# A list scheduler for two graph layers on one core: other durations, delays and port rules, hence another order of the same instructions

## The chip, the core and the metric

The kernel runs on one core of a Trainium2 chip. The core has a matrix engine (TensorE, in the profile PE, with its weight loads on a line of their own, PEld), a vector engine (VectorE, DVE), a scalar engine with activation functions (ScalarE, ACT), a general engine (GpSimd, POOL) and a sync engine (SyncE, SP), which here issues the transfers. Each engine runs its own list of instructions in order; semaphores make one wait for another. The metric is the device time in microseconds of one execution; the median of three runs of the kernel before is 2105.4 us (2105.02 to 2105.88).

## What is computed

There are 128 graphs of 128 nodes with 256 features each, x of shape (128, 128, 256) in f32, and an adjacency matrix of integers per graph. Two layers follow each other, each with a LayerNorm and ReLU ahead of it and a residual around it. The first is a gated graph network of three steps, the second a graph attention:

```python
# layer 0
h = relu(layernorm(x)); A = (adj != 0)
for i in range(3):
    m    = h @ weight[i]
    aggr = einsum('bst,bsd->btd', A, m)
    gi, gh = aggr @ w_ih.T + b_ih, h @ w_hh.T + b_hh      # three gates each
    r, z = sigmoid(i_r + h_r), sigmoid(i_z + h_z)
    n    = tanh(i_n + r * h_n)
    h    = (1 - z) * n + z * h
x = x + h
# layer 1
h = relu(layernorm(x)); Wh = h @ W; s = Wh.sum(-1)
e = leaky_relu(s[:, :, None] + s[:, None, :], 0.2); e = where(adj == 0, -inf, e)
x = x + softmax(e) @ Wh
```

## The kernel before, in words

**Tiling.** Four graphs make a group, and there are 32 groups. A group passes three phases, one for each step of the gated network, and then the attention. The list `turns` (L897 to L902) fixes the order of the phases; in the steady state it is (g, 0), (g − 1, 1), (g − 2, 2), so that three groups are under way at once. Three phases make a period.

**A phase.** The weights of a step are multiplied into w_ih beforehand, so the edge sums act on h itself: h is split into three bf16 parts, and `edge_sums` multiplies them with the adjacency matrix (L623, 12 bf16 matmuls of 128x128 for each half of the features), and ACT copies the sums out of the PSUM bank as `aT` (L626). The gate products use a fast multiplication scheme with seven products of halves: `node_sums` forms sums of halves, `hs` from the state on POOL and `gs` from the edge sums on DVE (L666 to L670), and `products` forms the seven products for two kinds of gates (`rz` and `n`) in six PSUM banks `x_`, `y_` and `q_`. In steps 0 and 1 a product is made of 128x256 matmuls (`product`, L697), in step 2, where rows come out directly, of 128x384 ones (`product_rows`, L711). `products` writes their order out: x (1), q (5), y (6), y (7), x (2), y (4), q (3), each for `rz` and then for `n`; in step 2 the middle numbers differ. Between them ACT copies banks out with `put` (L743; L747 and L749 where a bias is added), and DVE adds q to those copies with `add` (L753). The bank y_rz is such a loop: product (6) on it, ACT's copy L743 of it, then product (7) on the same bank; y_n (6) lies between. `gru` (L799 to L823) and `gru_rows` (L849 to L893) turn the sums into gates and the new state.

**Transposes.** Where the other layout of the state is needed, ACT copies halves of the f32 words into `pl` (L559) or `pe` (L1163), SP issues a transposing transfer, and ACT copies the result back (L563).

**Attention.** It is spread over the phases of later groups: e from the scores (L1022, L1040, or L1044 and L1046), exponentials on ACT (L1055), transposes, the weighted sums of rows (`weighted`, L652), the product with W (L1088) and the division and the residual on DVE (L1097). The last two groups have forms of their own (L993 to L1015, L1073, L1120 to L1149).

**The planner.** All of that is recorded first: `Plan.op` takes an engine, a duration in ns, the function that emits the instructions, and the buffers read and written. `Plan.run` is a list scheduler. It gives every operation a rank (its due time less durations and lags on the way there), and then places one operation after another on a clock for each engine: each time it takes the engine whose operation can start earliest, and among those the lowest rank. The gate products have due times, and their order among themselves is fixed (`bound`); all other TensorE work is put between them where it fits. A result becomes visible on another engine `LAG` ns after its end; DVE operations marked `two` and all of POOL's exclude each other in a reckoned `port`. The clocks serve only to find an order: at the end the operations are emitted in the order in which they were placed, and the engines run them as fast as their semaphores let them.

The functions that the change touches are these:

Of the kernel before, what the change touches and what calls it, by code (L numbers as in the profile page):

```python
# [13 lines left out]
OP = mybir.AluOpType  # L14
# [27 lines left out]
class Plan:  # L42
# [7 lines left out]
    LAG = {"PE": 250, "ACT": 300, "DVE": 300, "POOL": 300, "SP": 4000}  # L50
# [20 lines left out]
    def op(self, eng, ns, fn, reads=(), writes=(), room=(), due=None, mark=None,  # L71
           turn=None, two=False, lag=None):
# [24 lines left out]
        for b in free:  # L97
# [3 lines left out]
                           two or eng == "POOL", self.LAG[eng] if lag is None else lag])  # L101
# [4 lines left out]
        if turn is not None:  # L106
            self.turns.append((i, turn))

    def run(self):
# [29 lines left out]
        def rank_all():  # L139
            for i in reversed(topo):  # L140
                eng, ns, due = nodes[i][0], nodes[i][1], nodes[i][5]
                gap = 0 if i in bound else MARGIN
                rank[i] = min([due] + [rank[u] - (0 if nodes[u][0] == eng != "SP" else nodes[i][7])
                                       - (gap if u in bound else 0) for u in after[i]]) - ns
# [15 lines left out]
        clock, port = dict.fromkeys(self.LAG, 0.0), 0.0  # L160
# [3 lines left out]
        while len(order) < len(nodes):  # L164
            best = None
            for e, pool in ready.items():
# [3 lines left out]
                for i in pool:  # L170
                    if i in bound and i != chain[-1]:
                        continue
                    t = max(clock[e], at[i], port if nodes[i][6] else 0.0)
# [5 lines left out]
                    starts.append((t, i))  # L179
                first = min((t for t, _ in starts), default=float("inf"))  # L180
                if first == float("inf"):
                    continue
                i = min((i for t, i in starts if t <= first), key=lambda i: (rank[i], i))
                if best is None or first < best[0]:
                    best = (first, e, i)
            t, e, i = best
# [4 lines left out]
            clock[e] = t + n[1]  # L191
            if n[6]:
                port = clock[e]
            end = max(end, clock[e])
            for b in n[4]:
# [6 lines left out]
                b.done = max(getattr(b, "done", 0.0), clock[e] + n[7])  # L202
                if not b.left:
                    slots[b.tag][b.slot[1]] = b.done
            for u in users[i]:
                missing[u] -= 1
                at[u] = max(at[u], clock[e] + (0 if nodes[u][0] == e != "SP" else n[7]))
# [8 lines left out]
def kernel(  # L216
# [281 lines left out]
    def normed(src, dst, lo=0, hi=G):  # L498
# [3 lines left out]
        for b in range(lo, hi):  # L502
            op("DVE", 415, lambda b=b: nc.vector.bn_stats(ap(st)[:, b, :], ap(src)[:, b, :]),
               [(src, b, b + 1)], [(st, b, b + 1)])
# [4 lines left out]
        op("DVE", 160 * (hi - lo), aggr, [st], [mv])  # L509

        def rstd():
# [3 lines left out]
        op("DVE", 170, lambda: nc.vector.scalar_tensor_tensor(  # L515
            ap(nm)[:, part], ap(mv)[:, part, 0], -1.0, ap(rs)[:, part], op0=OP.mult, op1=OP.mult),
           [mv, rs], [nm])
        for b in range(lo, hi):
            op("ACT", 520, lambda b=b: nc.scalar.activation(
# [31 lines left out]
    def turned_halves(src, rows, dst):  # L551
# [5 lines left out]
        for k in range(KD):  # L557
# [5 lines left out]
            op("ACT", 1340, lambda k=k: nc.scalar.copy(  # L563
# [3 lines left out]
    def transpose(pl, plT, k, n):  # L567

        op("SP", 100, lambda: nc.sync.dma_start_transpose(
            ap(plT)[:, k, 0:n].rearrange("p c (m q) -> p (c m) q", q=P),  # L570
            ap(pl)[:, k, 0:n].rearrange("p c m -> p (c m)")), [(pl, k, k + 1)], [(plT, k, k + 1)],
           lag=4500)

    def parts_of(rows):
# [3 lines left out]
        for n in range(2):  # L578
            part = slice(2 * n, 2 * n + 2)
            op("POOL", 1106, lambda part=part: nc.gpsimd.tensor_tensor(  # L580
                ap(r1)[:, part], ap(rows)[:, part], top(rows)[:, part], OP.subtract),
               [(rows, 2 * n, 2 * n + 2)], [(r1, n, n + 1)])
            op("POOL", 1050, lambda part=part: nc.gpsimd.tensor_tensor(  # L583
# [5 lines left out]
    def turned_parts(hT):  # L589
# [6 lines left out]
        for k in range(KD):  # L596
# [3 lines left out]
            op("POOL", 1150, lambda k=k, r=r: nc.gpsimd.tensor_tensor(  # L600
# [4 lines left out]
            op("POOL", 1150, lambda k=k, r=r: nc.gpsimd.tensor_tensor(  # L605
# [5 lines left out]
    def edge_sums(parts, a, dst):  # L611
# [5 lines left out]
        for k in range(KD):  # L617
# [7 lines left out]
            op("PE", 700, edges, reads(k) + [a], [ps], [dst])  # L625
# [18 lines left out]
    def weighted(m, a, dst, lo, hi, homes):  # L644

        n, cols = hi - lo, slice(lo * N, hi * N)
        for k in range(KD):
# [7 lines left out]
            op("PE", 225 * n, sums, [(m, lo, hi), (a, lo, hi)], [ps], [dst])  # L655
# [60 lines left out]
    def products(layer, hT, hs, aT, gs, rows=False):  # L716
# [23 lines left out]
        def put(t, y, bias=None, mark=None):  # L740
# [9 lines left out]
            op("ACT", 760, halves, [y, W["bias_n"]], [t], mark=mark)  # L750
# [37 lines left out]
    def gru(layer, hT, hs, aT, gs):  # L788
# [7 lines left out]
        for j, n, src in blocks:  # L796
            cr, cz, cn, i = j, KD + j, 2 * KD + j, 2 * j + n
            s_rz, nn = src["rz"], src["n"]
            op("ACT", 511, lambda j=j, n=n, s_rz=s_rz, c=cr: nc.scalar.activation(  # L799
                view(rz, 0)[:, j, n, :], ap(s_rz)[:, 0, :], AF.Tanh, bias=ap(W["bias_s"])[:, c:c + 1],  # L800
                scale=0.5), [s_rz, W["bias_s"]], [(rz, i, i + 1)])
            if src is X:
                op("DVE", 290, lambda j=j, n=n: nc.vector.tensor_scalar(
                    view(rz, 0)[:, j, n, :], view(rz, 0)[:, j, n, :], 1.0, None, op0=OP.add),
                   [], [(rz, i, i + 1)])
                op("DVE", 480, lambda j=j, n=n, nn=nn: nc.vector.scalar_tensor_tensor(
                    view(u)[:, j, n, :], ap(nn)[:, 0, :], ap(W["bias_n"])[:, 0:1], view(rz, 0)[:, j, n, :],
                    op0=OP.add, op1=OP.mult), [nn, (rz, i, i + 1), W["bias_n"]], [(u, i, i + 1)])
            else:
                op("DVE", 480, lambda j=j, n=n, nn=nn: nc.vector.scalar_tensor_tensor(  # L810
# [6 lines left out]
            op("ACT", 500, lambda j=j, n=n, s_rz=s_rz, c=cz: nc.scalar.activation(  # L817
# [18 lines left out]
    def gru_rows(layer, hT, hs, aT, gs, rows, x1):  # L836
# [6 lines left out]
        for j, n, src in blocks:  # L843
            i = 2 * n + j
            outs = slice(j * P, (j + 1) * P)
            for m, bank in enumerate((src["rz"], src["n"])):
                graph, unit_of = 2 * n + m, 2 * i + m
                sbuf = bank.tag[0] == "t"
                op("ACT", 390, lambda outs=outs, graph=graph, bank=bank: nc.scalar.activation(  # L849
# [3 lines left out]
                op("DVE", 290, lambda outs=outs, graph=graph, bank=bank: nc.vector.scalar_tensor_tensor(  # L853
# [4 lines left out]
                op("DVE", 290, lambda outs=outs, graph=graph, bank=bank: nc.vector.scalar_tensor_tensor(  # L858
                    view(u)[:, graph, outs], view(u)[:, graph, outs], 0.5, flat(bank)[:, 3 * P:4 * P],
                    op0=OP.mult, op1=OP.add), [bank], [(u, unit_of, unit_of + 1)], two=sbuf)  # L860
        for n in (1, 0):
# [5 lines left out]
            tanh = [723, lambda cols=cols: nc.scalar.activation(  # L867
# [19 lines left out]
            op("POOL", 1290, lambda cols=cols, part=part: nc.gpsimd.tensor_tensor(  # L887
# [20 lines left out]
    def group(g):  # L908
# [4 lines left out]
        for t, src, kb in ((rows0, x[graphs].rearrange("b n d -> n b d"), 512),  # L913
# [3 lines left out]
            else:  # L917
                op("SP", 100, lambda t=t, src=src: nc.sync.dma_start(ap(t), src), [], [t])
        op("DVE", 420, lambda: nc.vector.tensor_scalar(ap(a), ap(at), 0.0, None,
                                                       op0=OP.not_equal), [at], [a])  # L920
        plan.due = (phase(g, L - 1) + 2) * SLOT
        normed(rows0, rows0)
        for layer in range(L):
# [9 lines left out]
            else:  # L933
# [3 lines left out]
                op("SP", 100, lambda: nc.sync.dma_start(  # L937
                    ap(x1), x[graphs].rearrange("b n d -> n b d")), [], [x1])
            hs, aT, gs = buf("hs"), buf("aT"), buf("gs")
            node_sums(hT, hs, "POOL", 1390, 940)  # L940
            edge_sums(parts, a, aT)
            node_sums(aT, gs, "DVE", 690, 440)
# [12 lines left out]
    def edges_of(g, a):  # L955

        e = buf("e")
        op("DVE", 415, lambda: nc.vector.tensor_scalar(
            ap(e), ap(a), 0.0, -BIG, op0=OP.is_equal, op1=OP.mult), [a], [e])
        return e, (buf("s_all") if g >= NG - ENDING else e)  # L960

    def attention(g, scores, x1, h1, lo, hi):
# [8 lines left out]
        for b in range(lo, hi):  # L971
            hw = buf("hw")
            op("DVE", 520, lambda b=b, hw=hw: nc.vector.scalar_tensor_tensor(
# [65 lines left out]
        if ending:  # L1039
            op("DVE", cost, lambda: nc.vector.tensor_reduce(small(top), sums(), AX.X, OP.max), units, [top])  # L1040
            op("DVE", 260, bound, [s], [top, low])
            op("ACT", 320 * n, leaky, [s] + units, [(e, lo, hi)])
# [17 lines left out]
        op("ACT", (400 if ending else 320) * n, exps, [low],  # L1060
# [143 lines left out]
```

## Time and profile before

| what | value |
|---|---|
| runs, median of three | 2105.4 us |
| profiled execution, span from the first to the last instruction | 2103.8 us |
| TensorE busy | 2084.5 us (99%), 10,624 matmuls and transposes |
| DVE busy | 1714.1 us (81%) |
| ACT busy | 1612.9 us (77%) |
| POOL busy | 923.7 us (44%) |
| mean granted TensorE clock | 0.998 of full speed |
| transfers | 65 GB/s in the mean |
| rows load, issue to landing | 4.2 us (median of 32) |
| transposing transfers `plT`, issue to landing | 3.3 us (median of 186) |

Busy times are sums of instructions as they lie in the trace; consecutive matmuls overlap in it, so a busy TensorE is not one at its peak. The page's row of forty digits gives the busy share of each fortieth of the span in tenths (52.6 us each). A line of a timeline gives the start in us from the span's start, the busy time in us, the engine, the line of the kernel, the operation, output and inputs by name, the shape, and how many such instructions follow each other; in brackets stands how long the engine was idle just before, and what it was waiting for.

### The profile page before, as it was taken

The numbers are of one execution on the slowest core, as the hardware profiler recorded it, in microseconds if no ns is written. First come the engines' busy times: TensorE is split into PE (matmuls) and PEld (weight loads), VectorE is DVE, ScalarE is ACT, GpSimd is POOL, SyncE is SP. The second block draws the span as 40 slices with busy tenths as digits, with TensorE's granted clock in tenths as the row PEclk, the third lists the DMA queues.
The fourth block names the chain that finished last, engine by engine and source line by source line (L and its number), as shares of the span: only waits on it lengthen the run. The fifth ranks groups of instructions, "written<-read, shape, count | busy, mean of one in ns | idle before, by whom it ended". The sixth has DMA issues, their size and how long they took to land.

```text
span 2103.8 us, 30718 instructions
## 1 busy us (share of the span) xinstructions
PE 2084.5 (99%) x10624; PEld 1661.6 (79%) x10624; DVE 1714.1 (81%) x3626; ACT 1612.9 (77%) x2977; POOL 923.7 (44%) x881
## 2 busy tenths in 40 slices
PE   8999999999999999999999999999999999999998
PEld 6886887777887778887778877778877788688765
DVE  6767888788888888888888887888878978778788
ACT  5577887877878787877778777778787777677676
POOL 4544554344443435543444543444444454335330
PEclk9999999999999999999999999999999999999999
DMA  4322323322233222323223233222323222312231
GB/s 131 61 51 48 56 54 81 67 54 61 68 73 81 60 58 65 72 70 76 61 56 70 68 73 68 54 61 68 74 61 85 45 62 71 76 41 61 56 71 41
DMA packets 365148, 137.02 MB, mean 65 GB/s; under 512 B 296384, under 2 KB 364736, under 8 KB 364992
## 3 DMA queue, kind: packets, MB, share of 16 engines
q1 hardware_dynamic: 364992, 135.05, 28.8%
q8 instruction: 84, 1.38, 0.3%
q14 instruction: 72, 0.59, 0.1%
HBM read 45.36 MB, written 16.78 MB: 30 GB/s over the span
## 4 chain that ended last, share of the span: by engine, by line
PE 94%; DVE 3%; ACT 1%; DMA 1%; issue 0%; SPq 0%; DVEq 0%; ACTq 0%
PE y_rz L697 15%; PE q_rz L697 10%; PE x_rz L697 10%; PE y_n L697 8%; PE misc L623 6%; PE y_n L711 5%; PE y_rz L711 5%; PE x_n L697 5%; PE q_n L697 5%; PE misc L1088 5%; PE q_rz L711 4%; PE x_n L711 4%; PE x_rz L711 4%; PE q_n L711 4%; PE misc L652 3%; PE misc L452 0%
## 5 line engine op out<-in xcount | busy, mean ns | idle before, releaser
L580 POOL TENSOR_TENSOR r<-rows 128x512 f32<-128x512 f32 x126 | 139.7, 1129 | 295.9 <-ACT rows L563 201.7
L743 ACT COPY t_rz<-y_rz 128x512 f32<-128x512 f32 x192 | 112.5, 586 | 130.4 <-PE y_rz L697 91.8
L666 POOL TENSOR_TENSOR hs<-hT 128x512 f32<-128x512 f32 x96 | 126.6, 1319 | 190.7 <-PE y_n L711 110.9
L753 DVE TENSOR_TENSOR t_rz<-t_rz,q_rz 128x512 f32<-128x512 f32 x192 | 131.5, 685 | 86.5 <-ACT t_rz L743 43.5
L697 PE MATMUL y_rz<-hs,s_hh 128*128 128x256 f32 x768 | 197.4, 379 | 0.6 <-ACT t_rz L743 0.5
L697 PE MATMUL y_rz<-gs,s_x 128*128 128x256 f32 x768 | 197.1, 379 | 0.0
L670 POOL TENSOR_TENSOR hs<-hT,hs 128x256 f32<-128x256 f32 x96 | 77.5, 807 | 209.6 <-PE q_n L711 169.2
L697 PEld LDWEIGHTS y_rz<-gs,s_x 128*128 128x128 f32 x768 | 145.9, 190 | 19.8
L605 POOL TENSOR_TENSOR pl<-d,pl 128x512 bf16<-128x512 f32 x64 | 76.1, 1193 | 191.9 <-ACT pl L603 191.7
L697 PEld LDWEIGHTS y_rz<-hs,s_hh 128*128 128x128 f32 x768 | 143.5, 190 | 20.0 <-ACT t_rz L743 1.4
L583 POOL TENSOR_TENSOR p<-r 128x512 bf16<-128x512 f32 x126 | 156.7, 1262 | 0.0
L753 DVE TENSOR_TENSOR t_n<-t_n,q_n 128x512 f32<-128x512 f32 x192 | 131.2, 683 | 30.4 <-PE q_n L711 13.0
L666 DVE TENSOR_TENSOR gs<-aT 128x512 f32<-128x512 f32 x96 | 87.8, 914 | 54.3 <-ACT aT L626 53.7
L697 PE MATMUL x_rz<-aT,s_x 128*128 128x256 f32 x512 | 131.4, 379 | 0.0
L697 PE MATMUL x_rz<-hT,s_hh 128*128 128x256 f32 x512 | 131.4, 379 | 0.0
L600 POOL TENSOR_TENSOR d<-hT,pl 128x512 f32<-128x512 f32 x64 | 82.6, 1293 | 97.2 <-ACT pl L598 91.5
L626 ACT COPY aT<-misc 128x512 f32<-128x512 f32 x190 | 110.4, 586 | 17.7 <-PE misc L623 13.0
L1088 PE MATMUL misc<-w,uT 128*128 128x256 f32 x480 | 115.1, 383 | 3.1 <-DVE x L1097 2.3
L697 PE MATMUL y_n<-hs,s_hh 128*128 128x256 f32 x384 | 114.3, 379 | 0.0
L697 PE MATMUL y_n<-gs,s_x 128*128 128x256 f32 x384 | 114.2, 379 | 0.0
L697 PEld LDWEIGHTS x_rz<-hT,s_hh 128*128 128x128 f32 x512 | 97.2, 190 | 19.3
L887 POOL TENSOR_TENSOR x<-x,u 128x512 f32<-128x512 f32 x60 | 79.4, 1342 | 69.8 <-DMA x<-in_x_dram 42.1
(286 smaller groups left out, 6324.4 us busy)
## 6 DMA issues: line engine op xcount, KB each, us to landing
rows<-in_x_dram SPq DMA_DIRECT2D x32, 512.0 KB, 4.2
x<-in_x_dram SPq DMA_DIRECT2D x32, 512.0 KB, 3.9
out_dram<-x SPq DMA_DIRECT2D x31, 512.0 KB, 2.9
at<-in_adj_dram SPq DMA_DIRECT2D x32, 256.0 KB, 2.8
plT<-pl SPq DMA_TRANSPOSE x186, 3.3
peT<-pe SPq DMA_TRANSPOSE x60, 3.1
e<-in_L_gnn_weight_dram SPq DMA_DIRECT2D x3, 256.0 KB, 3.1
rz<-in_L_gnn_w_ih_dram SPq DMA_DIRECT2D x2, 384.0 KB, 4.3
```

The lines of the kernel that those rows point to most:

```text
L580: op("POOL", 1106, lambda part=part: nc.gpsimd.tensor_tensor(ap(r1)[:, part], ap(rows)[:, part], top(rows)[:, part], OP.subtract), [(rows, ...
L583: op("POOL", 1050, lambda part=part: nc.gpsimd.tensor_tensor(ap(p3)[:, part], ap(r1)[:, part], top(r1)[:, part], OP.subtract), [(r1, n, n ...
L600: op("POOL", 1150, lambda k=k, r=r: nc.gpsimd.tensor_tensor(ap(r), ap(hT)[:, k], part(pl, k, 0), OP.subtract), [(hT, 2 * k, 2 * k + 2), (p ...
L623: nc.tensor.matmul(flat(ps)[:, b * N:(b + 1) * N], part(i, b, k), ap(a)[:, b, :], start=(i == 0), stop=(i == 2))
L626: op("ACT", 590, lambda k=k, ps=ps: nc.scalar.copy(ap(dst)[:, k, :], flat(ps)), [ps], [(dst, 2 * k, 2 * k + 2)])
L666: op(eng, cost, lambda: sub(ap(w)[:, 0:2, :], blocks()[:, 1::2, :], blocks()[:, 0:2, :], OP.subtract), [t], [(w, 0, 2)], two=True)
L697: nc.tensor.matmul(ap(bank)[:, half, :], ap(w)[:, i - 1, gate, :], source(i, t, sums), start=(first and c == 0 and m == 0), stop=False, sk ...
L711: op("PE", 645, lambda c=c, w=w, t=t, sums=sums: nc.tensor.matmul(flat(bank)[:, c * P:(c + 3) * P], source(i, t, sums)[:, m * N:(m + 1) * ...
L743: op("ACT", 590, lambda: nc.scalar.copy(ap(t), ap(y)), [y], [t], mark=mark)
L753: op("DVE", 690, lambda: nc.vector.tensor_tensor(ap(t), ap(t), ap(q), OP.add), [q], [t])
L887: op("POOL", 1290, lambda cols=cols, part=part: nc.gpsimd.tensor_tensor(part(x1), part(x1), ap(u)[:, cols], OP.add), [(u, 2 * lo, 2 * hi)] ...
L1088: nc.tensor.matmul(ap(ps)[:, b, :], ap(uT)[:, k, (m + b) * N:(m + b + 1) * N], ap(w1)[:, k, :], start=(k == 0), stop=(k == KD - 1))
```

## The change

No instruction is added or removed. `Plan` reckons with other numbers:

- The durations of many operations are other numbers of ns, and four more DVE operations count as users of the port (`two=True`).
- The lag of an operation is split: `LAG` belongs to the producer, `SIGNAL` to the engine that waits; between two TensorE operations there is none. SP's transfers get 480 ns on the queue (transposes 1,283), a lag of 3,600 (transposes 2,200).
- `OVER` lets the next operation of the same engine begin before the end of the one before it.
- An f32 product behind a `thin` operation (the bf16 edges) starts `FLIP` = 56 ns later.
- The port is handed on `HANDOFF` = 120 ns before the end of its user.
- A released buffer can be used 36 ns later, and of two engines that could start something equally early, the one is taken whose operation asked first.

```diff
-    LAG = {"PE": 250, "ACT": 300, "DVE": 300, "POOL": 300, "SP": 4000}
+    LAG = {"PE": 163, "ACT": 0, "DVE": 0, "POOL": 0, "SP": 3600}
+    OVER = {"PE": 0, "ACT": 103, "DVE": 84, "POOL": 42, "SP": 0}
+    FLIP, HANDOFF = 56, 120
+    SIGNAL = {"PE": 53, "ACT": 36, "DVE": 36, "POOL": 78, "SP": 28}
...
+    def wait(self, i, u):
+        a, b = self.nodes[i], self.nodes[u][0]
+        return 0 if a[0] == b == "PE" else a[7] + self.SIGNAL[b]
...
-                rank[i] = min([due] + [rank[u] - (0 if nodes[u][0] == eng != "SP" else nodes[i][7])
+                rank[i] = min([due] + [rank[u] - self.wait(i, u)
                                        - (gap if u in bound else 0) for u in after[i]]) - ns
...
-                    t = max(clock[e], at[i], port if nodes[i][6] else 0.0)
+                    t = max(clock[e] + (self.FLIP if thin and e == "PE" and not nodes[i][8] else 0), at[i])
...
-                    starts.append((t, i))
-                first = min((t for t, _ in starts), default=float("inf"))
+                    starts.append((max(t, port) if nodes[i][6] else t, t, i))
+                first = min((t for t, _, _ in starts), default=float("inf"))
...
-                i = min((i for t, i in starts if t <= first), key=lambda i: (rank[i], i))
-                if best is None or first < best[0]:
-                    best = (first, e, i)
+                asked, i = min(((r, i) for t, r, i in starts if t <= first), key=lambda x: (rank[x[1]], x[1]))
+                if best is None or (first, asked) < best[:2]:
+                    best = (first, asked, e, i)
...
-            clock[e] = t + n[1]
+            done = t + n[1]
+            clock[e] = done - self.OVER[e]
             if n[6]:
-                port = clock[e]
-            end = max(end, clock[e])
+                port = done - self.HANDOFF
+            if e == "PE":
+                thin = n[8]
...
-                b.done = max(getattr(b, "done", 0.0), clock[e] + n[7])
+                b.done = max(getattr(b, "done", 0.0), done + n[7] + 36)
...
-                at[u] = max(at[u], clock[e] + (0 if nodes[u][0] == e != "SP" else n[7]))
+                at[u] = max(at[u], done + self.wait(i, u))
```

Of the operations, a few that stand for all:

```diff
-        op("SP", 100, lambda: nc.sync.dma_start_transpose(
+        op("SP", 1283, lambda: nc.sync.dma_start_transpose(
...
-           lag=4500)
+           lag=2200)
...
-            op("PE", 700, edges, reads(k) + [a], [ps], [dst])
+            op("PE", 671, edges, reads(k) + [a], [ps], [dst], thin=True)
...
-            op("ACT", 760, halves, [y, W["bias_n"]], [t], mark=mark)
+            op("ACT", 728, halves, [y, W["bias_n"]], [t], mark=mark)
...
-            tanh = [723, lambda cols=cols: nc.scalar.activation(
+            tanh = [630, lambda cols=cols: nc.scalar.activation(
...
-            node_sums(hT, hs, "POOL", 1390, 940)
+            node_sums(hT, hs, "POOL", 1272, 730)
...
-            op("ACT", 400, lambda b=b: exps(b, b + 1), [low], [(e, b, b + 1), (den, b, b + 1)])
+            op("ACT", 480, lambda b=b: exps(b, b + 1), [low], [(e, b, b + 1), (den, b, b + 1)])
```

## The prediction

> **What bounds the kernel now.** I read the page from the top, then the waits of TensorE, the span cut into forty windows, and the timelines of TensorE, ScalarE (ACT) and VectorE (DVE) around each wait. On the page:
>
> ```profile
> span 2103.8 us, 30718 instructions
> PE 2084.5 (99%) x10624; PEld 1661.6 (79%) x10624; DVE 1714.1 (81%) x3626; ACT 1612.9 (77%) x2977; POOL 923.7 (44%) x881
> PE   8999999999999999999999999999999999999998
> PE 94%; DVE 3%; ACT 1%; DMA 1%; issue 0%; SPq 0%; DVEq 0%; ACTq 0%
> ```
>
> TensorE is busy in 99% of the span and carries 94% of the chain that ended last. What it does can't change, so the question is only how much time is not matmuls at full pace. Busy time can't tell that: the Trainium skill ("Perfetto Trace Analysis", Identifying the Most-Contended Engine) says that pipelined matmuls make matmul busy time a bad measure. So I take spacings from start to start in the timeline. At full pace they are 0.2156 us for 128x256 f32, 0.3225 for 128x384, 0.0556 for the bf16 edge matmuls, 0.111 for 128x128 f32; the skill ("TensorE: Matmul & The Clock Gate", Wait — 56ns, not 53.3ns?) gives 55.6 and 215.7 ns for the first two kinds, and the trace agrees. All 10,624 spacings at these values make 2059.5 us. The other 44.4 of the 2103.8 are: 5.7 ahead of the first and after the last matmul's start; 8.4 in 149 changes from bf16 to f32, median 0.056; about 30 in waits and slow stretches (9.0 start-up, 1.3 at 157–221 us, 1.35 at 1659–1772, 8.3 at 1799–1812, 1.3 at 1998–2051, 7.1 in the end, 2.2 in crumbs). From 430 to 1500 us nothing waits. The runs' median, 2105.4, lies 1.6 above the span; I work on the span and add 1.6.
>
> A bf16-to-f32 change in the TensorE timeline (first number start, second busy): after edges, two starts take 0.70, elsewhere 0.65.
>
> ```profile
> 1791.05 0.86 PE L711 MATMUL q_n<-s_x,gs 128*128 128x384 f32 x2
> 1791.75 0.81 PE L711 MATMUL y_rz<-s_hh,hs 128*128 128x384 f32 x2
> 1792.40 0.81 PE L711 MATMUL y_rz<-s_x,gs 128*128 128x384 f32 x2
> ```
>
> The big hole, same view:
>
> ```profile
> 1797.35 1.89 PE L1088 MATMUL misc<-w,uT 128*128 128x256 f32 x8
> 1801.59 3.65 PE L1088 MATMUL misc<-w,uT 128*128 128x256 f32 x8 [2.35 <-DVE x L1097]
> 1807.26 0.91 PE L711 MATMUL y_n<-s_hh,hs 128*128 128x384 f32 x2 [2.03 <-ACT t_n L743]
> 1808.72 1.48 PE L711 MATMUL x_rz<-s_hh,hT 128*128 128x384 f32 x2
> ```
>
> Two idles of 2.5 and 2.4 us (with the hand-over), and behind each some matmuls at half pace: eight in 3.65 instead of 1.89 (+1.7), then five of 0.64 instead of 0.32 (+1.6). The skill (the same page, Part 1: The HAM clock gate) says the clock halves after an idle window of about 3.4 us that runs free; here 2.35 idle was enough. What is late there is DVE: a row of 128x512 that takes 0.69 us took 1.53 twice (L1044, L1046), L668 took 1.14 instead of 0.43, while POOL worked. "SBUF — State Buffer" (Who interferes with whom) says that a DVE instruction with two SBUF inputs and a reading GpSimd instruction exclude each other for a whole instruction; these rows fit.
>
> Lastly the place where gate products have no other work between them: y_rz (product 6), y_n (6), y_rz (7). ACT copies y_rz out (L743) while y_n runs, and y_rz goes on:
>
> ```profile
> 180.60 0.59 PE L697 MATMUL y_n<-gs,s_x 128*128 128x256 f32 x2
> 181.03 1.10 PE L697 MATMUL y_rz<-hs,s_hh 128*128 128x256 f32 x4
> ...
> 221.35 1.13 PE L697 MATMUL y_rz<-hs,s_hh 128*128 128x256 f32 x4
> 222.32 1.03 PE L697 MATMUL y_rz<-gs,s_x 128*128 128x256 f32 x4
> ```
>
> Copy on time: four matmuls busy for 1.10 instead of 1.03, so about 0.08 lost. At 221.35 ACT came 0.22 late (it had just begun a 1.04 copy, L1163), and 0.20 + 0.10 were lost: after a stop the second pass pays 0.1 more. Before has two such bare loops in 64 phases; everywhere else edges, attention or sums stand between.
>
> **The change, part by part.** The instructions are the same in number and kind; only their order differs. I read the order that the changed planner writes (an order, without times), counted TensorE's work at the spacings above, and the other engines' at their rows' lengths less what successive instructions overlap.
>
> 1. *Changes of type* (the 56 ns that the planner now charges an f32 product behind `thin` edges). It puts edges one behind another: 149 changes become 97 or 98. 51 x 0.056 = −2.9.
>
> 2. *Bare loops* (PE's lag 250 becomes 163 + 36, ACT's 300 becomes 0 + 53). Four products are planned at 0.864 us; the old numbers wanted 250 + 590 + 300 = 1,140 ns for the copy between, so the planner put fillers there; the new want 842, so it fits. Bare y_rz–y_n–y_rz loops go from 2 to 35. Each has 4 matmuls x 0.2156 = 0.86 from y_n's first start, 1.079 from the last start on y_rz; needed are 0.415 to ACT's start, 0.586 for the copy, 0.053 back = 1.054. Slack: 25 ns. With ACT free, 33 x 0.08 = +2.6. In the steady pattern ACT's queue ahead of that copy is 3.80 us of work from its last forced start (L743 0.48, L1163 0.95, L747 0.37, L749 0.27, L563 1.20, L867 0.53), 0.51 before it is needed. Windows of 1.3 to 2.0 us (y_n to y_n, row products, the attention's L1097) also become more frequent, with 0.4 or more of slack: 0, covered by that slack; a third of them 0.1 late would cost 4.
>
> 3. *Fill.* At 201–203 us ACT put seeds (L738) before two evictions: 0.43 + 0.23 + 2 x 0.10 = 0.86 lost. In the new order enough stands between: −0.9.
>
> 4. *The hole and the stretch before* (port sharing, measured DVE and ACT times). Before: 1.2 at 1765–1772 (an y_rz wait 0.68 + 0.10, gs 0.39) and 8.3, 9.4 together. In the new order the nearest squeeze is ahead of an y_rz (7) at about 1756 us of TensorE's work: ACT has L563, four L519, L747, L749, L559, L823 and the t2 copies in front of L743. Added up, they end 2.3 to 3.0 us after TensorE needs them; a wait of 0.33 stands just before. I take 2.6 + 0.3 + 0.4 for second passes + 1.7 for one halved clock = 5.0, so −4.4. Bounds: hole as large as before (0), or no halving and little left (−7).
>
> 5. *Edges behind their transpose.* The planner's 1283 + 2200 makes 3.48 us; the timeline shows 3.1–3.2 from issue to landing for two planes and about 3.65 for three. Once (about 1875 us of work) only 2.2–2.5 us of TensorE's work stand between: +1.3. "DMA: Bandwidth & Descriptors" (Anatomy of one DMA) puts a fixed 2 us on completion; the transposes here show more. A queue change on SP costs nothing while loads have phases of slack; where one is late, as the rows load of 6.1 us (usual 4.2) before the hole, it belongs to item 4's bounds.
>
> 6. *2004–2014 us.* Edges follow edges on one bank, nothing between: 0.83 + 0.10, and gs 0.26 + 0.10; before lost 1.0 here: +0.3.
>
> 7. *The end.* TensorE's work ahead of the last gate product shrinks by 2.4: the 2.9 of item 1 less 0.45 of attention matmuls (L1015) drawn ahead; so item 1's −2.9 is replaced by −2.4. After that product before needs 28.6 us, with DVE nearly full. The new order has done these DVE pieces ahead of it: L1022 0.72, L1040 0.72, one L871 0.72, one L753 0.60, L958 0.31, L1035–1038 about 0.2, some 3.3; it puts four L1097 (0.4 each) before the second half's chain, of which I let 0.6 count: −2.7 (bounds −1.0, −4.4).
>
> 8. *Start-up.* Fillers are re-ordered round DMA waits: 0, hidden behind the weight loads (0.9 and 1.3 us waits stay); the 1.6 at 30.6 us (L533) may go, or a new one come: −1.5 to +1.
>
> Sum: −2.4 + 2.6 − 0.9 − 4.4 + 1.3 + 0.3 − 2.7 = −6.2. Span 2103.8 − 6.2 = 2097.6; with 1.6, 2099.2 us.
>
> **Rivals.**
> - *A, slower: ACT is late at the bare loops.* Speaks for it: slack of 25 ns, and one of before's two was 0.22 late at a cost of 0.30. Against: the 0.51 counted. With 0.22 late everywhere, 33 x 0.30 = 9.9 in place of 2.6: 2106.5, no change. If one L749 copy (0.36) stands in front, 0.36 − 0.025 + 0.10 = 0.44 each, 14.5: 2111.1. It decides from about 0.31 late (+10.4 over 2099.2).
> - *B, no change: the hole only moves.* For it: its causes (a slow load, POOL holding DVE, a halved clock) are only partly what the planner reckons with. Item 4 at 0: 2103.6.
> - *C, no change: TensorE is saturated and only the type changes count*: 2105.4 − 2.9 = 2102.5. Against it: 30 us of waits that lie in places which the order moves.
> - *D, clearly faster*: hole and end at their better bounds (−7, −4.4): 2099.2 − 2.6 − 1.7 = 2094.9, with start-up 2093.4.
> - That the change does nothing is out: the order differs on every engine.
>
> **How the numbers follow.** 0.2% (4.2 us) is about what a measurement of this kernel can tell from no change. The forecast 0.40, own range 2095.5 to 2101.2; D 0.14; B and C together 0.28; A 0.18, half of it above 2110.5. So faster 0.54, same 0.28, slower 0.18. The range 2092.5 to 2110.5 leaves out half of A and the tip of D.
>
> **What would show it.** In the changed profile: 97 or 98 type changes; some 35 bare loops with y_rz rows of x4 at about 1.10 us (1.03 would mean item 2 costs nothing, 1.3 or more is A); no wait at 201–203; near 1760–1790 one wait of TensorE on L743 of 2 to 3 us and rows at half pace after it (none: D; two: B); one wait of an L623 on a transpose near 1890; less than 28.6 us after the last L711 row. The prediction falls if waits appear in the middle of the span, where before has none, or if DVE, with its lengthened rows beside POOL, comes late for the y_n and q products that I set at 0.

## The result, and the profile after

The changed kernel takes 2124.7 us (median of four runs, 2123.9 to 2125.2) against 2105.2 for the kernel before: the ratio is 1.0095, with a 95% interval of 1.0082 to 1.0109. It is slower by about 20 us, and outside the forecast's range. Of the two profiled executions the spans are 2123.4 and 2103.8 us, 19.6 apart.

The head of the page after, in the same order as before:

```profile
span 2123.4 us, 30792 instructions
PE 2087.9 (98%) x10624; PEld 1657.5 (78%) x10624; DVE 1694.1 (80%) x3626; ACT 1595.9 (75%) x2977; POOL 929.7 (44%) x881
PE   8999999999999999999999999999999999999998
```

DVE and ACT are busy for less time than before (1694 and 1596 us against 1714 and 1613), and the row of forty digits looks as it did: a loss of 1% is spread too thinly for it. The view of TensorE's waits shows it at once (columns: us in total, times, longest):

```profile
PE y_rz L708 <- ACT t_rz L754: 17.8, 22, 3.4
PE misc L663 <- DVE x L1108: 1.6, 4, 0.5
PE misc L663 <- ACT aT L637: 1.4, 2, 0.9
```

Lines below the planner are 11 higher than before: L708 is L697, L754 is L743. The first row stood at 0.5 us, once, before. Twenty of its 22 waits are the bare loop of the prediction, with ACT's copy of y_rz between products 6 and 7; the longest, 3.4 us, is the hole shown below. The groups of instructions say the same; here `18.1` is TensorE's idle time ahead of that group, which was 0.6 before:

```profile
L708 PE MATMUL y_rz<-hs,s_hh 128*128 128x256 f32 x768 | 201.9, 385 | 18.1 <-ACT t_rz L754 17.8
```

One period of the steady state in the timeline of TensorE (start, busy time):

```profile
1052.84 1.03 PE L708 MATMUL y_rz<-gs,s_x 128*128 128x256 f32 x4
1053.70 0.59 PE L708 MATMUL y_n<-hs,s_hh 128*128 128x256 f32 x2
1054.13 0.59 PE L708 MATMUL y_n<-gs,s_x 128*128 128x256 f32 x2
1055.36 1.13 PE L708 MATMUL y_rz<-hs,s_hh 128*128 128x256 f32 x4 [0.63 <-ACT t_rz L754]
```

y_n's four matmuls fill 0.86 us, then TensorE stands still for 0.63. The spacings from start to start give the account. There are 35 bare loops. Fifteen, up to 429 us and from 1725 on, lost 0.08 each. The other twenty, between 303 and 1575 us, came late: 17.4 us over pace (beyond the steady spacings) at the first matmul after the wait and 20 x 0.104 in the second pass, 19.5 us. That is about as much as the difference of the spans; what else changed nearly cancels (changes of type cost 2.8 us less, the other waits and the fifteen loops some 3 us more).

The hole near 1800 us is still there, 3.4 us of idle and then half pace, at another place:

```profile
1797.78 2.08 PE L708 MATMUL y_rz<-hs,s_hh 128*128 128x256 f32 x4 [3.41 <-ACT t_rz L754]
1799.65 1.91 PE L708 MATMUL y_rz<-gs,s_x 128*128 128x256 f32 x4
```

**Why ACT is late.** Followed back from the wait at 1055.36, ACT ran without a pause from 1048.71 until it reached the copy at 1054.73. Lines of its timeline (in brackets idle time and what ended it):

```profile
1046.04 2.08 ACT L530 ACTIVATE h<-x,nm,rs 128x256 f32<-128x256 f32 x4 [0.45 <-DVE nm L526]
1048.02 0.40 ACT L860 ACTIVATE rz<-t_rz 128x256 f32<-128x256 f32 x1
1048.71 0.42 ACT L860 ACTIVATE rz<-t_n 128x256 f32<-128x256 f32 x1 [0.29 <-DVE t_n L764]
...
1050.76 0.62 ACT L754 COPY y_rz<-x_rz 128x512 f32<-128x512 f32 x1
...
1054.73 0.58 ACT L754 COPY t_rz<-y_rz 128x512 f32<-128x512 f32 x1
```

Just before that it had waited twice for DVE: for nm, four numbers in each partition, and for t_n. DVE and POOL at that time:

```profile
1044.78 1.22 DVE L526 SCALAR_TENSOR_TENSOR nm<-mv,rs 128x4 f32<-128x4 f32 x1 [0.45 <-POOL rs L524]
1046.13 0.81 DVE L869 SCALAR_TENSOR_TENSOR u<-u,t_rz 128x128 f32<-128x128 f32 x1
1048.01 0.67 DVE L764 TENSOR_TENSOR t_n<-t_n,q_n 128x512 f32<-128x512 f32 x1
```

```profile
1043.73 1.02 POOL L524 TENSOR_TENSOR rs<-rs,neghalf 128x4 f32<-128x4 f32 x1
1044.72 1.27 POOL L677 TENSOR_TENSOR hs<-hT 128x512 f32<-128x512 f32 x1
1046.06 0.73 POOL L679 TENSOR_TENSOR hs<-hs,hT 128x256 f32<-128x256 f32 x1
```

nm takes 1.22 us instead of 0.15, and ends just as POOL's L677 ends, which had begun 0.06 before it. L869 takes 0.81 instead of 0.28 in the same way beside L679. In the numbers that the planner itself writes down as it orders, L677 starts 7.1 us ahead of the y_n product; on the chip it started 9.0 ahead (1044.72 against 1053.70), 1.9 us too soon, and DVE's t_n came 1.0 late. This gave two theories to test: (1) the loss sits in the bare loops, which the planner makes because its hand-over delays say they fit; (2) ACT is late there because POOL's hs sum takes the port sooner than planned.

### The profile page after: what moved, and what is told of

It reads as the page before. It is cut to its first block, busy times and chain, and to the rows that moved or that the text cites. A ratio compares the mean times of both kernels' runs of the same rounds, so it can differ in the third digit from the quotient of the medians.

```text
span 2123.4 us, 30792 instructions
## 1 busy us (share of the span) xinstructions
PE 2087.9 (98%) x10624; PEld 1657.5 (78%) x10624; DVE 1694.1 (80%) x3626; ACT 1595.9 (75%) x2977; POOL 929.7 (44%) x881
## 5 line engine op out<-in xcount | busy, mean ns | idle before, releaser
L591 POOL TENSOR_TENSOR r<-rows 128x512 f32<-128x512 f32 x126 | 149.7, 1207 | 291.0 <-ACT rows L574 179.8
L708 PE MATMUL y_rz<-hs,s_hh 128*128 128x256 f32 x768 | 201.9, 385 | 18.1 <-ACT t_rz L754 17.8
L708 PE MATMUL y_rz<-gs,s_x 128*128 128x256 f32 x768 | 198.0, 380 | 0.0
L677 POOL TENSOR_TENSOR hs<-hT 128x512 f32<-128x512 f32 x96 | 133.3, 1389 | 141.4 <-PE y_n L722 75.9
L708 PEld LDWEIGHTS y_rz<-hs,s_hh 128*128 128x128 f32 x768 | 142.7, 190 | 49.1 <-ACT t_rz L754 30.3
L611 POOL TENSOR_TENSOR d<-hT,pl 128x512 f32<-128x512 f32 x64 | 77.4, 1211 | 214.0 <-DVE hT L843 189.0
L754 ACT COPY t_rz<-y_rz 128x512 f32<-128x512 f32 x192 | 111.9, 583 | 72.9 <-PE y_rz L708 44.7
L708 PEld LDWEIGHTS y_rz<-gs,s_x 128*128 128x128 f32 x768 | 146.5, 191 | 20.1
L708 PE MATMUL x_rz<-aT,s_x 128*128 128x256 f32 x512 | 131.4, 379 | 0.0
L708 PE MATMUL x_rz<-hT,s_hh 128*128 128x256 f32 x512 | 131.4, 379 | 0.0
L837 DVE TENSOR_TENSOR d<-hT,u 128x512 f32<-128x512 f32 x128 | 94.4, 739 | 43.8 <-ACT u L834 38.6
L637 ACT COPY aT<-misc 128x512 f32<-128x512 f32 x190 | 106.3, 582 | 29.3 <-PE misc L634 27.1
L677 DVE TENSOR_TENSOR gs<-aT 128x512 f32<-128x512 f32 x96 | 99.3, 1035 | 34.5 <-ACT aT L637 32.7
L708 PE MATMUL y_n<-hs,s_hh 128*128 128x256 f32 x384 | 114.9, 381 | 0.0
L708 PE MATMUL y_n<-gs,s_x 128*128 128x256 f32 x384 | 114.6, 380 | 0.0
L834 ACT ACTIVATE u<-u,bias_i 128x512 f32<-128x512 f32 x128 | 92.3, 722 | 28.5 <-DVE u L825 28.3
L708 PEld LDWEIGHTS x_rz<-hT,s_hh 128*128 128x128 f32 x512 | 97.3, 190 | 19.4
```

The costliest lines, as they stand in the source:

```text
L591: op("POOL", 1042, lambda part=part: nc.gpsimd.tensor_tensor(ap(r1)[:, part], ap(rows)[:, part], top(rows)[:, part], OP.subtract), [(rows, ...
L637: op("ACT", 590, lambda k=k, ps=ps: nc.scalar.copy(ap(dst)[:, k, :], flat(ps)), [ps], [(dst, 2 * k, 2 * k + 2)])
L677: op(eng, cost, lambda: sub(ap(w)[:, 0:2, :], blocks()[:, 1::2, :], blocks()[:, 0:2, :], OP.subtract), [t], [(w, 0, 2)], two=True)
L708: nc.tensor.matmul(ap(bank)[:, half, :], ap(w)[:, i - 1, gate, :], source(i, t, sums), start=(first and c == 0 and m == 0), stop=False, sk ...
L754: op("ACT", 590, lambda: nc.scalar.copy(ap(t), ap(y)), [y], [t], mark=mark)
L834: op("ACT", 723, lambda j=j, cols=cols: nc.scalar.activation(ap(u)[:, cols], ap(u)[:, cols], AF.Tanh, bias=ap(W["bias_i"])[:, 2 * KD + j:2 ...
```

## The experiments

Each ratio is taken to the kernel before as it ran beside that kernel on the same chip. "Over pace" means the sum, in the one profiled execution, of what start-to-start spacings of TensorE exceed the steady ones by, without changes of type and without excesses under 8 ns. Single executions of the kernel before lay between 2099.8 and 2107.7 us in one series, so a few microseconds between two spans, or two sums over pace, mean nothing by themselves; the ratios decide.

| kernel | median us | ratio to before, 95% interval | span of the profile | over pace |
|---|---|---|---|---|
| before | 2105.2 | 1 | 2103.8 | 28.4 |
| changed | 2124.7 | 1.0095 (1.0082–1.0109) | 2123.4 | 50.8 |
| one delay put back, 300 ns | 2094.0 | 0.9959 (0.9945–0.9974) | 2092.7 | 20.4 |
| hs's first column waited for | 2117.9 | 1.0075 (1.0058–1.0092) | 2115.6 | 42.8 |
| all old delays | 2090.0 | 0.9943 (0.9929–0.9958) | 2087.5 | 15.2 |
| before with type changes charged | 2099.6 | 0.9988 (0.9980–0.9997) | 2097.6 | 24.3 |
| POOL's hs sums read nothing | 2099.2 | 0.9979 (0.9972–0.9987) | 2096.8 | 24.3 |
| all of hs waited for | 2103.5 | 1.0000 (0.9991–1.0009) | 2100.9 | 28.5 |
| one delay, 24 ns | 2095.9 | 0.9960 (0.9945–0.9974) | 2092.2 | 19.7 |
| before with the new durations | 2111.5 | 1.0034 (1.0022–1.0046) | 2107.5 | 32.1 |
| before with the new delays | 2105.5 | 1.0011 (1.0004–1.0018) | 2105.1 | 30.0 |
| before with overlap and early port | 2097.3 | 0.9966 (0.9955–0.9978) | 2097.1 | 22.0 |
| old delays, 200 for 300 | 2089.4 | 0.9930 (0.9912–0.9948) | 2089.6 | 16.7 |

**One delay put back.**

```diff
-                op("ACT", 590, lambda: nc.scalar.copy(ap(t), ap(y)), [y], [t], mark=mark)
+                op("ACT", 590, lambda: nc.scalar.copy(ap(t), ap(y)), [y], [t], mark=mark, lag=300)
...
-            op("ACT", 728, halves, [y, W["bias_n"]], [t], mark=mark)
+            op("ACT", 728, halves, [y, W["bias_n"]], [t], mark=mark, lag=300)
```

> The changed planner, except that the copies out of y_rz and y_n (put) again get 300 ns until TensorE may use the bank (the changed planner gives 53). By the plan, bare y_rz-y_n-y_rz loops fall from 35 to 2, type changes stay at 96. Theory 1 (the loss sits in the bare loops: 22 waits of 17.8 us in all, 0.26 more for each in its first two passes, and 0.08 for each of the 13 that were on time): some 20 us come back, 2101 to 2106 us. Rival (ACT's lateness of 0.7 us is the harm, the bare loop only its first collector): TensorE waits at other narrow windows instead, 2110 us or more.

Measured: 2094.0, below both expected ranges. The twenty waits are gone, as theory 1 has it; between 450 and 1900 us one wait above 0.3 is left, 0.8 at 1663. The halved pace near 1800 us is gone too. But the edit moved the rest of the order as well, and nm is hardly held up any more: 332 ns in the mean of its 65 instructions, against 656 in the changed kernel, and 0.17 us at 1049.43, in the steady state. This run takes away the bare loops and most of ACT's lateness together, so by itself it doesn't refute the rival. The run with the new delays alone, further down, has late inputs for ACT and no bare loops.

**The same with 24 ns.** The planned loop is 163 + 36 + 590 + 53 = 842 ns against 864 for the four products. 20 ns more leave 34 bare loops in the plan, 24 leave 2.

```diff
-                op("ACT", 590, lambda: nc.scalar.copy(ap(t), ap(y)), [y], [t], mark=mark)
+                op("ACT", 590, lambda: nc.scalar.copy(ap(t), ap(y)), [y], [t], mark=mark, lag=24)
...
-            op("ACT", 728, halves, [y, W["bias_n"]], [t], mark=mark)
+            op("ACT", 728, halves, [y, W["bias_n"]], [t], mark=mark, lag=24)
```

> The changed planner with 24 ns more than it reckons (0) for the copies out of y_rz and y_n, which makes the planned loop 866 ns against four products of 864. By the plan: 2 bare y_rz-y_n-y_rz loops in place of 35, 96 type changes. Theory 1 (knife edge: what fits by 22 ns in the plan loses 20 us on the chip): 2090 to 2098 us, like 300 ns. Rival (300 ns helped since it pushed ACT's copies and their readers apart in general): between 2100 and 2120 us.

Measured: 2095.9. TensorE's timeline has the row products in the place of the wait:

```profile
1045.66 0.59 PE L708 MATMUL y_n<-gs,s_x 128*128 128x256 f32 x2
1046.09 1.89 PE L1099 MATMUL misc<-w,uT 128*128 128x256 f32 x8
1047.82 1.03 PE L708 MATMUL y_rz<-hs,s_hh 128*128 128x256 f32 x4
```

So 24 ns in the planner's arithmetic are worth some 28 us on the chip (0.9960 against 1.0095). About 20 of them are the loops'; in this order the hole near 1800 us is gone as well. 24 ns do nearly as much as 300: it isn't the size of the delay that helps, but whether the loop fits.

**POOL made to wait: first column.** The order of the changed kernel is kept in this and the next two runs.

```diff
+        def first():
+            if eng == "POOL":
+                nc.gpsimd.memset(ap(w)[:, 3, 0:1], 0.0)
+            sub(ap(w)[:, 0:2, :], blocks()[:, 1::2, :], blocks()[:, 0:2, :], OP.subtract)
-        op(eng, cost, lambda: sub(ap(w)[:, 0:2, :], blocks()[:, 1::2, :], blocks()[:, 0:2, :],
-                                  OP.subtract), [t], [(w, 0, 2)], two=True)
+        op(eng, cost, first, [t], [(w, 0, 2)], two=True)
```

> The order of the changed kernel, untouched; only POOL writes one element of the hs slice that TensorE reads last before it forms the next hs, so that POOL starts as late as the planner believes (after the whole old hs is read) and not as early as the semaphores allow. Theory 2 (ACT is late because POOL's hs sum takes the shared port 1.9 us ahead of plan, so that DVE's small nm takes 1.22 us instead of 0.15, and ACT's normalisation and its tanh inputs come 0.6 to 1.0 late): the waits on y_rz of 0.63 us each shrink to nothing or nearly, 2104 to 2110 us. Rival (durations and overlaps of ACT are set too short in themselves): the waits stay, 2122 to 2126 us.

Measured: 2117.9, between the two ranges. The waits of 0.63 became 0.65 in the steady state, and two of 1.1 us at 303 and 367 went. In the timeline POOL's write stands at 1041.95 and the hs sum at 1042.01, directly behind L524, while the q_n product that reads the last hs columns ran from 1042.76: the first column is read by the q_rz product before it, and held nothing up. nm took 1.26 us again. This run can't speak against theory 2, since it didn't hold POOL back. The hole near 1800 us was smaller (2.7 us of idle), for which no cause was looked for.

**POOL made to wait: last column.** As above, with

```diff
-                nc.gpsimd.memset(ap(w)[:, 3, 0:1], 0.0)
+                nc.gpsimd.memset(ap(w)[:, 3, H - 1:H], 0.0)
```

> As the run with one element of hs written first, but the element lies in the last column, which the n product reads; the first column was free 0.65 us after POOL came to it or sooner, and so held nothing up. Now POOL's hs sum can start only after the whole old hs is read, as the planner has it. Theory 2: nm takes 0.15 us again, and ACT's normalisation starts 0.6 us sooner; if POOL then starts no sooner than planned, the waits on y_rz go (2103 to 2110 us); if POOL still takes the port ahead of DVE's sum t_n, which it can since nothing orders the two, half of each wait stays (2110 to 2116 us). Rival (ACT's own durations): 2116 us or more.

Measured: 2103.5, at the edge of the better range: the whole loss is back, though one POOL instruction per phase was added and nothing was taken away or moved. DVE, POOL and ACT in one period:

```profile
1035.51 0.16 DVE L526 SCALAR_TENSOR_TENSOR nm<-mv,rs 128x4 f32<-128x4 f32 x1 [0.44 <-POOL rs L524]
```

```profile
1037.11 0.10 POOL L680 MEMSET hs<- 128x1 f32 x1 [1.64 <-PE q_n L726]
1037.17 1.43 POOL L681 TENSOR_TENSOR hs<-hT 128x512 f32<-128x512 f32 x1
```

```profile
1036.22 2.07 ACT L530 ACTIVATE h<-x,nm,rs 128x256 f32<-128x256 f32 x4
1038.20 0.41 ACT L864 ACTIVATE rz<-t_rz 128x256 f32<-128x256 f32 x1
1038.50 0.41 ACT L864 ACTIVATE rz<-t_n 128x256 f32<-128x256 f32 x1
...
1044.64 0.58 ACT L758 COPY t_rz<-y_rz 128x512 f32<-128x512 f32 x1
```

and TensorE's bare loop, with no wait:

```profile
1045.30 1.11 PE L712 MATMUL y_rz<-hs,s_hh 128*128 128x256 f32 x4
```

POOL now idles 1.64 us until q_n has read hs, nm takes 0.16, ACT goes through both its inputs without a gap. Only three waits on y_rz are left (3.8 us with the hole's 2.7). So the planner's picture of this buffer was at fault: it holds a buffer until its last reader, while the semaphores release each hs slice with that slice's own last reader. The hs sum could run sooner than planned, and did, in the wrong place.

**POOL's hs sums read nothing.** Zeros are written where the sums would stand, so the computation lacks them; the order is the changed kernel's.

```diff
+        if eng == "POOL":
+            op(eng, cost, lambda: nc.gpsimd.memset(ap(w)[:, 0:2, :], 0.0), [t], [(w, 0, 2)], two=True)
+            op(eng, half, lambda: nc.gpsimd.memset(ap(w)[:, 2, :], 0.0), [t, (w, 1, 2)], [(w, 2, 3)], two=True)
+            op(eng, half, lambda: nc.gpsimd.memset(ap(w)[:, 3, :], 0.0), [t, (w, 2, 3)], [(w, 3, 4)], two=True)
+            return
```

> The order of the changed kernel, untouched, but POOL's three hs sums are replaced by writes of zeros over the same hs slices, so that they read nothing (the sums over the state are left out of the computation, and the output is not the reference's). Theory 2 (POOL's hs sums, which read SBUF, hold back DVE's instructions with two SBUF inputs, DVE is then 0.6 to 1.0 us late with nm and with the sum t_n, and ACT with it): in the steady state nm takes about 0.15 us instead of 1.22, and the 17 waits on y_rz of about 0.63 us shrink to 0 to 0.2: 2103 to 2110 us. Rival (ACT's own durations and overlaps are reckoned too short): the waits stay at 0.5 us or more, 2117 us or more.

Measured: 2099.2, below the range of theory 2. One wait on y_rz is left, the hole's 2.8 us. The write and nm side by side:

```profile
1033.00 0.52 POOL L678 MEMSET hs<- 128x512 f32 x1
```

```profile
1033.08 0.16 DVE L526 SCALAR_TENSOR_TENSOR nm<-mv,rs 128x4 f32<-128x4 f32 x1 [0.44 <-POOL rs L524]
```

POOL starts as early as in the changed kernel, but a POOL instruction that only writes doesn't hold nm up. That is what the Trainium skill ("SBUF — State Buffer", Who interferes with whom) says of a DVE instruction with two SBUF inputs: it contends with a GpSimd instruction that reads SBUF, not with one that only writes. It is also shorter (0.52 for 1.27), but nm was through at 1033.24, before the write's end at 1033.52. With the run before it, theory 2 stands.

**All old delays.**

```diff
-    LAG = {"PE": 163, "ACT": 0, "DVE": 0, "POOL": 0, "SP": 3600}
+    LAG = {"PE": 250, "ACT": 300, "DVE": 300, "POOL": 300, "SP": 4000}
...
-    SIGNAL = {"PE": 53, "ACT": 36, "DVE": 36, "POOL": 78, "SP": 28}
+    SIGNAL = dict.fromkeys(LAG, 0)
...
-        return 0 if a[0] == b == "PE" else a[7] + self.SIGNAL[b]
+        return 0 if a[0] == b != "SP" else a[7] + self.SIGNAL[b]
...
-                b.done = max(getattr(b, "done", 0.0), done + n[7] + 36)
+                b.done = max(getattr(b, "done", 0.0), done + n[7])
```

> The changed planner with the old hand-over delays (PE 250, ACT, DVE and POOL 300, SP 4000 where no own lag is given, nothing for the waiting engine, nothing for a buffer's release) and all else new: durations, overlaps, type changes, port. Bare loops by the plan: 2. Theory 1: 2100 to 2106 us, as with the one delay put back alone. Rival (the overlaps and durations make the order brittle everywhere): above 2112 us.

Measured: 2090.0, below the expected range and better than both kernels. Over pace are 15.2 us, of which 8.5 lie in the first 53 us and 5.4 in the last two fortieths; between 430 and 1700 us no spacing is over pace by 0.1 or more, and there is no hole. The other parts of the change, taken together, help then, once the delays keep their margin.

**The same with 200 for 300** (PE stays at 250).

> As the run with old delays, but ACT, DVE and POOL at 200 ns in place of 300. By the plan: 1 bare loop, 99 changes of type, an end 5.5 us earlier. If reality follows the plan: 2083 to 2088 us, the fastest version here. Theory 1 (what the plan gains by tighter windows is lost on the chip): no better than 300, 2089 to 2096 us.

```diff
-    LAG = {"PE": 250, "ACT": 300, "DVE": 300, "POOL": 300, "SP": 4000}
+    LAG = {"PE": 250, "ACT": 200, "DVE": 200, "POOL": 200, "SP": 4000}
```

Measured: 2089.4. The planner's end is 5.5 us earlier, the chip's isn't: the profiled spans are 2089.6 and 2087.5. The two can't be told apart by their intervals, as theory 1 has it. It is the fastest median here, by 0.7% under before.

**Parts of the change alone, on the kernel before.** Type changes:

```diff
-                    t = max(clock[e], at[i], port if nodes[i][6] else 0.0)
+                    t = max(clock[e] + (56 if thin and e == "PE" and not nodes[i][8] else 0), at[i], port if nodes[i][6] else 0.0)
...
-            op("PE", 700, edges, reads(k) + [a], [ps], [dst])
+            op("PE", 700, edges, reads(k) + [a], [ps], [dst], thin=True)
```

> The kernel before with one part of the change alone: an f32 product behind bf16 edges is planned 56 ns later. By the plan 148 changes of type become 114. If only those count: 34 x 0.056 = 1.9 us less, 2103.5 us. If each shift of the edges moves waits elsewhere as well: anything from 2100 to 2112, with the number of type changes in the trace nonetheless about 114.

Measured: 0.9988. The trace has 115 changes of type, 6.5 us in place of 8.4; 1.9 us is what was forecast; the ratio makes 2.5 us, by its interval 0.6 to 4.2. The waits moved all the same: 24.3 us over pace, with other places than before.

Durations: all the new numbers of ns and the four new port members, under the old `Plan`; two of them stand for all.

```diff
-            op("ACT", 760, halves, [y, W["bias_n"]], [t], mark=mark)
+            op("ACT", 728, halves, [y, W["bias_n"]], [t], mark=mark)
...
-            node_sums(hT, hs, "POOL", 1390, 940)
+            node_sums(hT, hs, "POOL", 1272, 730)
```

> The kernel before with the new durations and port members alone; delays, overlaps, type changes and hand-over as before. By the plan: 3 bare loops, 151 changes of type. If the durations removed the hole of 8 us near 1800 us and the other waits: 2094 to 2098 us. If that took the overlaps or the port's hand-over: the hole stays, 2100 to 2108 us.

Measured: 1.0034, slower, which neither reading expected. The hole is there (2.8 and 1.9 us of idle near 1800), and two waits of 2.8 and 3.1 us come at 2033 and 2061. The new durations are longer than the old ones in some places and shorter in others; which number does it was not tried.

Delays: `LAG`, `SIGNAL`, `wait` and the 36 ns of the change, under the old durations.

```diff
-    LAG = {"PE": 250, "ACT": 300, "DVE": 300, "POOL": 300, "SP": 4000}
+    LAG = {"PE": 163, "ACT": 0, "DVE": 0, "POOL": 0, "SP": 3600}
+    SIGNAL = {"PE": 53, "ACT": 36, "DVE": 36, "POOL": 78, "SP": 28}
...
-                at[u] = max(at[u], clock[e] + (0 if nodes[u][0] == e != "SP" else n[7]))
+                at[u] = max(at[u], clock[e] + self.wait(i, u))
```

> The kernel before with the new hand-over delays alone (163 + 53, 0 + 36 and so on, 36 for a release), old durations, no overlap, no charge for a change of type. By the plan: 8 bare y_rz-y_n-y_rz loops, 147 changes of type. Theory 1 says that the delays do the harm through bare loops: 8 loops at 0.08 to 0.9 are 0.6 to 7 us, and narrow windows elsewhere come on top: 2104 to 2114 us. Rival (the short delays are right, and only hurt together with the shorter engine times): 2098 to 2103 us.

Measured: 1.0011, 2105.5 us, in the range of theory 1. The group of nm in this run and in the kernel before (busy time in all, mean ns):

```profile
L521 DVE SCALAR_TENSOR_TENSOR nm<-mv,rs 128x4 f32<-128x4 f32 (+1 forms) x65 | 51.1, 786 | 1.4 <-POOL rs L519 1.4
```

```profile
L515 DVE SCALAR_TENSOR_TENSOR nm<-mv,rs 128x4 f32<-128x4 f32 (+1 forms) x65 | 17.8, 275 | 2.7 <-POOL rs L513 2.7
```

nm is held up even longer than in the changed kernel (786 ns in the mean, there 656). Between 430 and 1600 us ACT waits 18 times for it, 16.8 us in all, and yet TensorE doesn't wait between 251 and 1800 us: there are 8 bare loops and not 35, and none of them lies there. This is what speaks against the rival of the first run. At one of the eight, at 226 us, the two come together:

```profile
PE y_rz L703 <- ACT t_rz L749: 5.1, 2, 4.0
```

TensorE waits 4.0 us there for ACT, which had itself waited 2.5 for DVE, whose L864 took 1.03 instead of 0.28 beside POOL's L589; with the half pace behind it that loop costs 6.7 us. So the even total hides a balance: the hole of the kernel before is gone, and this one has come. A late ACT does no harm without bare loops, and a bare loop little without a late ACT (the run in which all of hs is waited for).

Overlap and port hand-over (`OVER` and `HANDOFF`, under all the old numbers):

```diff
-            clock[e] = t + n[1]
+            done = t + n[1]
+            clock[e] = done - {"PE": 0, "ACT": 103, "DVE": 84, "POOL": 42, "SP": 0}[e]
             if n[6]:
-                port = clock[e]
+                port = done - 120
```

> The kernel before with overlap of successive instructions and the port handed on 120 ns early, and nothing else of the change. By the plan: 2 bare loops, 146 changes of type. If the gain of the run with old delays (16 us under before) comes from these two, since the plan no longer lets VectorE and ScalarE run behind the hardware: 2092 to 2099 us, with the 8 us hole near 1800 us smaller than 3. If it takes the measured durations as well: 2100 to 2106 us.

Measured: 0.9966. There is no hole near 1800, and 22.0 us over pace in place of some 28: this part alone brings 0.34% where the run with old delays brings 0.57%.

## Why the prediction was wrong

**The step that failed is item 2, bare loops, where it set ACT's margin at 0.51 us.** The count of loops (35), their arithmetic (1.054 needed of 1.079) and the price of a loop in time (0.08) came out as written, for fifteen of them. The queue's length was right as well: 3.80 us were reckoned from the copy out of x_rz to the copy out of y_rz, and the trace has 3.97 (1050.76 to 1054.73). What was wrong is where that sum starts. I let ACT begin 4.31 us ahead of the time at which TensorE's work allowed the copy, 1053.90; it began 3.14 ahead, since it had stood waiting for t_n, and t_n for a DVE held up by POOL. 1.17 later, less 0.51 of margin, plus 0.17 of length, makes 0.83 late. The formula of rival A, lateness − 0.025 + 0.10, gives 0.90 a loop, and the spacings 0.795 + 0.104 = 0.90. So rival A, ACT late at the bare loops, was right, and so was its price for a loop. It had 0.18, and it was priced with one copy of 0.36 in front at all loops; the real lateness was more than twice that, at twenty loops, and came from DVE and not from a copy. Its threshold (0.31) was not tried.

I had seen the cause in the kernel before (L1044 at 1.53 us instead of 0.69 beside POOL) and used it only for the hole. An order without times can't show it: nothing in it ties POOL's hs sum to DVE's nm, so the queue content of ACT alone was no bound for ACT.

**Item 1, type changes:** right; 98 of them, 5.6 us in place of 8.4.
**Item 3, fill:** right; no wait at 201–203 us.
**Item 4, the hole:** right in its place (a y_rz (7) behind ACT) and in the half pace, too small in size. It was priced at 5.0; the wait at 1797.8 cost 3.57, the half pace behind it 2.6, the one ahead 0.64 + 0.10, 6.9 in all, and one of 0.81 at 1741 came in. That makes about 8 where 9.4 stood before, a gain of some 1 where 4.4 was forecast. In the runs with one delay put back the idle and the half pace are gone.
**Item 5, edges behind their transpose:** right; one wait at 1921 us, 1.25 (forecast 1.3).
**Item 6:** too small; 1.02 and 0.84 at 2053–2062 where 0.83 and some 0.36 were written.
**Item 7, the end:** right in sign, inside its bounds; from the last gate product on 25.0 us in place of 28.6, a gain of 3.6 (forecast 2.7).
**Item 8, start-up:** about nothing (9.4 us in the first fortieth, 9.0 before).
**The narrow windows set at 0:** mostly right. Three sums behind the attention's L1108 cost 0.42, 0.59 and 0.62 at 641, 1289 and 1485 us, one y_rz 0.42 at 1312, and sums behind ACT's L637 0.71 at 1967.

Rivals B, C and D were wrong since all of them took the middle of the span for free of waits.

The 55.6 and 215.7 ns that the prediction quotes are stated by the Trainium skill ("TensorE: Matmul & The Clock Gate", Wait — 56ns, not 53.3ns?) for 128 and 512 columns. The trace agrees with the first (0.0556 us for 128 columns in bf16). The 0.2156 us for 256 columns in f32 only looks like the second; it and 0.3225 stand on this trace alone, and so do the sums.

## What to carry to other kernels

A planner's order is as good as the things it ties together: where two engines hold each other up but no semaphore orders them (here POOL's sum and DVE's nm, 0.06 us apart), the one that comes first goes first, whatever the plan had meant, and a buffer model coarser than the semaphores lets it come sooner than planned (here by 1.9 us). Where an engine is full, hand-over delays in a planner are margins; exact ones let loops through that fit by 22 ns, and each turns any lateness of the other engine into idle time. To forecast such a loop, begin the other engine's queue at its last real wait, found by following that queue back across engines, and not at the last time at which the full engine lets it start.

## What the runs showed of the hardware

- An instruction of 128x4 numbers on VectorE, about 0.16 us by itself, took 1.22 to 1.26 us when a reading GpSimd instruction of 1.27 had begun 0.02 to 0.06 before it; with a writing one of 0.52 beside it, it took 0.16.
- A wait of TensorE costs more than its idle time: with 0.63 us of idle, the spacing at that matmul was 0.795 over pace, and one in the next pass 0.104 more. The 0.16 in between is overlap lost: a matmul of 128x256 f32 is busy for 0.379 us, and at full pace the next one starts after 0.2156.
- After 3.4 us of idle, eleven matmuls of 128x256 came at twice their spacing (0.21 over 0.2156); after the 0.6 to 1.1 us waits none did. In between, the length of the idle doesn't decide alone: half pace followed 2.35 us in the kernel before and 2.7 in the run with all of hs waited for, and did not follow 2.5 with type changes charged (at 2055 us), nor 2.8 and 3.1 with the new durations (at 2033 and 2061).
